# Tables and ranks within the first convolution, moved group norm parts, and logit copies between the two exponentials of a step

## The chip, the cores and the metric

The kernel runs on one core of a Trainium2 chip, all in float32. The metric is the device time of one execution in microseconds (us); before the change the median of three runs is 3284.09 us (3280.82 to 3286.93). Five engines work beside each other, each on its own list of instructions in order: TensorE (PE; PEld is its weight load), VectorE (DVE), ScalarE (ACT), GpSimd (POOL) and SyncE (SP), which here only issues DMA transfers. They wait for each other through semaphores.

## What is computed

Eight images of 512 channels by 32 x 32 pixels. A first layer normalises x in 32 groups, runs a convolutional block with two attention stages, and adds x; a second layer normalises the result, multiplies by a masked 1x1 convolution with permuted output channels, and adds again. Cut to what matters (constants in numbers, reshapes left out):

```python
def layer0(x):                       # x = x + layer0(gn(x))
    t = silu(bn(conv1x1(x, cv1_w)))
    ys = [t[:, :256], t[:, 256:]]
    for i in range(2):
        z = silu(bn(conv3x3(ys[-1], m_cv1_w[i])))
        q, k, v = conv1x1(z, m_qkv_w[i])          # 4 heads of 64, 1024 positions
        a = softmax(einsum('bhdi,bhdj->bhij', q, k + (rw + rh)) / 8)
        z = einsum('bhij,bhdj->bhdi', a, v)
        ys.append(ys[-1] + silu(bn(conv1x1(z, m_cv2_w[i]))))
    return silu(bn(conv1x1(concat(ys), cv2_w)))

def layer1(x):                       # x = x + layer1(gn(x))
    s_hat, t_hat = softmax(S, 1), softmax(T, 1)   # 512 channels x 16 groups
    s, t = argmax(s_hat, 1), argmax(t_hat, 1)
    mask = t[:, None] == s[None, :]
    w_eff = conv * t_gain[:, None] * mask         # the gains are the largest entries
    dense = conv1x1(x * s_gain, w_eff)
    p = argsort(t, stable=True)
    return dense[:, p[p]]
```

## The kernel before

**Stages.** At the start, x of the first two images is loaded and normalised and goes through the first 1x1 convolution (`start_conv`, lines 930 to 942, called in lines 943 to 957). The 3x3 convolution of the first image follows (lines 962 to 968); each third step of it also runs a piece of the generator `last_weights` (lines 608 to 699), which prepares layer 1. Its pieces: the one-hot tables of S and T and their largest entries; `oht`, the transposed tables; the mask, multiplied into the convolution weights; `rank`, the place of each channel in the stable sort; a permutation matrix from it; and two rounds of matmuls that permute the weights. For `rank`, line 668 runs 5 + 6 + 7 + 8 = 26 matmuls of 16 columns, one chain for each block of 128 channels: all "lower group" counts of four blocks, the one-hot counts of the blocks before, and a triangle within the block.

**The attention.** It is split into 64 units: image, block, pair of heads, half of the positions. A unit has 8 key tiles t; for each, `logits` (line 487) multiplies k by q into two banks `lg`, ScalarE copies the banks into a tile `st` (line 500), and VectorE takes the running maximum `mx` (line 505). After the last tile `top` (line 507) transposes the maxima (`mt`) and `spread` (line 516) transposes the negated maxima back over the partitions (`mb`). Then `soften` (line 523) adds `mb` on VectorE (line 525), takes the exponential on ScalarE (line 526) and adds the tiles up on GpSimd (`sum`, line 531); `values` (line 533) multiplies by v into `po` (line 537). `finish` (line 545) sums over the partitions by `den` and divides (line 554).

**The loop** (lines 1004 to 1034) works in steps of two key tiles on two units at once: the exponentials and values of unit u, the logits of unit u + 1. One step emits `soften(t)`, `soften(t + 1)`, `values(t - 2)`, `values(t - 1)`, next unit's `logits(t)` and `logits(t + 1)`, and then `advance`: as much filler (convolutions of other images, projections) as the planner counts for the step. The next unit's logits take their `st` tiles from a pool of ten (`stp`), so a copy into one waits until the values matmul and the sum of its former user are done. Five PSUM banks (`ps_f`) serve logits and all filler.

**What sets the order.** Each engine gets its instructions in the order in which the program emits them, as far as a scheduler keeps it; `in_turn` (line 182) fixes the order of VectorE for the attention. Nothing fixes ScalarE's order. A clock of planned times (`Clock`, line 711) is advanced by the estimated microseconds of each emitted TensorE piece; `clock.at(d, f)` emits f when d planned us have passed.

**Group norm.** `GroupNorm` (lines 134 to 166) takes statistics on VectorE; `mean` (line 141) aggregates them (`mv`), averages over a group by a matmul with `gmat` (`gm`, line 146) and forms squares (`gd`); `var` (line 154) does the second matmul (`gv`, line 156), GpSimd takes the power (`gr`), VectorE the offset (`go`). ScalarE then normalises (line 165). These parts are placed by the clock: in `First.early` (line 755) 9 and 13 us after x of a later image is asked for, in `Second.body` (line 782) 11 and 16 us after an image's last matmul of layer 0.

**Small loads.** `small_parameters` (line 561) issues five small transfers from ScalarE's queue, in the order batch norm constants (`bn_sb`), `rw`, `rh`, S and T (`s_sb`), and VectorE prepares the batch norm factors `bn_s` and `bn_b`.

Of the kernel before, what the change touches and what calls it, by code (L numbers as in the profile page):

```python
# [39 lines left out]
def conv_preact_kernel(ctx: ExitStack, tc: tile.TileContext, x, cv1, cv2, mcv1, qkv, mcv2, bn, rw, rh, conv, s_in, t_in, out):  # L40
# [141 lines left out]
    def in_turn(instruction):  # L182

        if turn:
            tc.add_manual_dep(instruction.ins, turn.pop().ins.name, IN_ORDER, reason="order of VectorE")
        turn.append(instruction)

    class Spread:

# [288 lines left out]
    class Unit:  # L478
# [8 lines left out]
        def logits(self, t):  # L487

            if t == 0:
                self.begin()  # L490
            lg = [bank(f"lg_{self.name}_{t}_{h}") for h in range(2)]
            for h in range(2):
                r = slice(HD * h, HD * h + HD)
                nc.tensor.matmul(  # L494
                    lg[h], self.k[r, ts(t, P)], self.q[r, self.hp, ts(self.half, HALF)], start=True, stop=True
                )
            st = pair(stp, "st", f"st_{self.name}_{t}")
            self.st.append(st)
            for h in range(2):
                nc.scalar.copy(st[:, h], lg[h])  # L500
            if t == 1:
                self.mx = pair(one, "mx", f"mx_{self.name}")
            for h in range(2 if t else 0):
                so_far = self.st[0] if t == 1 else self.mx
                in_turn(nc.vector.tensor_tensor(self.mx[:, h], so_far[:, h], lg[h], ALU.max))  # L505
# [17 lines left out]
        def soften(self, t):  # L523
            st = flat(self.st[t])
            in_turn(nc.vector.tensor_tensor(st, st, flat(self.mb), ALU.add))  # L525
            nc.scalar.activation(st, st, AF.Exp)  # L526
            if t == 1:
                self.acc = pair(one, "acc", f"sum_{self.name}")
            for h in range(2 if t else 0):
                so_far = self.st[0] if t == 1 else self.acc  # L530
                nc.gpsimd.tensor_tensor(self.acc[:, h], so_far[:, h], self.st[t][:, h], ALU.add)  # L531
# [28 lines left out]

    def small_parameters():

        nc.scalar.dma_start(out=bn_sb, in_=bn)
        nc.scalar.dma_start(out=rw_sb, in_=rw)
        nc.scalar.dma_start(out=rh_sb, in_=rh)
        nc.scalar.dma_start(out=s_sb[:, 0], in_=s_in)
        nc.scalar.dma_start(out=s_sb[:, 1], in_=t_in)
        nc.vector.tensor_scalar_add(bn_b, bn_sb[:, 3], 1e-3)
        nc.gpsimd.tensor_tensor(bn_s, bn_b, mhalf, ALU.pow)
        nc.vector.tensor_tensor(bn_s, bn_s, bn_sb[:, 0], ALU.mult)  # L570
        nc.vector.tensor_tensor(bn_b, bn_sb[:, 2], bn_s, ALU.mult)
        nc.vector.tensor_tensor(bn_b, bn_sb[:, 1], bn_b, ALU.subtract)
# [35 lines left out]
    def last_weights():  # L608

        weff = [pair(stp, "st", f"weff_{j}") for j in range(2)]  # L610
        for j in range(2):
            load(weff[j], conv[:, 2 * j : 2 * j + 2])
        scr = flat(pair(stp, "st", "scr")).rearrange("p (a k g) -> p a k g", a=8, g=NG)
        gi = scr[:, 0]
        gi_i = scr[:, 7].bitcast(mybir.dt.int32)
        nc.gpsimd.iota(gi_i, pattern=[[0, 2 * CT], [1, NG]], base=-NG, channel_multiplier=0)
# [22 lines left out]
        nc.vector.tensor_tensor(oh, gi, wide(idx), ALU.is_equal)  # L639
        nc.vector.tensor_tensor(lower, gi, wide(idx), ALU.is_gt)  # L640

        yield
        oht = pair(stp, "st", "oht")[:NG]
        for a in range(2):
            ps = bank(f"oht_{a}")
            for k in range(CT):
                nc.tensor.transpose(ps[:NG, ts(k, P)], oh[:, CT * a + k], ident)
            nc.vector.tensor_copy(oht[:, a], ps[:NG])
        yield
        for k in range(CT):  # L650
            ps = bank(f"mask_{k}")
# [2 lines left out]
            stt(wk, wk, gain[:, CT + k : CT + k + 1], ps, ALU.mult, ALU.mult)  # L654

        yield

        tri = small.tile([P, P], F32, tag="tri", bufs=1, name="tri")
        nc.gpsimd.affine_select(
            out=tri, in_=ones, pattern=[[1, P]], compare_op=ALU.is_gt, fill=0.0, base=0, channel_multiplier=-1  # L660
        )
        rank = small.tile([P, CT], F32, tag="rank", bufs=1, name="rank")
        for k in range(CT):
            ps = bank(f"rank_{k}")
            terms = [(ones, lower[:, CT + c]) for c in range(CT)] + [(ones, oh[:, CT + c]) for c in range(k)]
            terms.append((tri, oh[:, CT + k]))
            for n, (w, rhs) in enumerate(terms):
                nc.tensor.matmul(ps[:, :NG], w, rhs, start=(n == 0), stop=(n == len(terms) - 1))
            nc.vector.tensor_tensor(e[:, k], ps[:, :NG], oh[:, CT + k], ALU.mult)
        nc.vector.tensor_reduce(rank, e[:, :CT], AX.X, ALU.add)  # L670

        io = pair(stp, "st", "io")
        io_i = io[:, 1].bitcast(mybir.dt.int32)
        nc.gpsimd.iota(io_i, pattern=[[1, HALF]], base=0, channel_multiplier=0)
# [76 lines left out]
    class First(Item):  # L751
# [4 lines left out]
        def early(self):  # L756
            if self.h == 0:
                self.im.measure_x()
                clock.at(9.0, self.im.gn0.mean)
                clock.at(13.0, self.im.gn0.var)  # L760
                self.im.normed = clock.now + 13.0

        def setup(self):
            self.tiles = self.im.load_x(self.h)
# [8 lines left out]
    class Second(Item):  # L773
# [8 lines left out]
        def body(self):  # L782
            yield from self.im.conv2(self.h, self.tiles)
            if self.h == 1:
                clock.at(11.0, self.im.gn1.mean)
                clock.at(16.0, self.im.gn1.var)
                self.im.normed = clock.now + 16.0
                self.im.measured = True
                bg.prepare()

# [160 lines left out]
    clock.at(9.0, second.gn0.var)  # L951
    clock.at(11.0, lambda: start_norm(second, tiles2))
    clock.at(12.0, lambda: transform_weights(0))
    clock.run(start_conv(first, tiles, w))
    first.load_y()
    bg.add(*(First(m, h) for m in images[2:] for h in range(2)))
# [2 lines left out]
    positions(0)  # L959
    bg.prepare()  # L960
    first.transform(0, 0.0, 0.0)
    side = last_weights()
    for n, us in enumerate(first.conv3(0)):
        clock.tick(us)
        if n % 3 == 0:
# [15 lines left out]
    for s in range(len(slots)):  # L981
# [22 lines left out]
        for j in range(4):  # L1004
# [91 lines left out]
```

## Time and profile before

| | |
|---|---|
| median of three runs | 3284.09 us (3280.82 to 3286.93) |
| profiled execution, its own time | 3278.47 us |
| its span in the trace | 3276.7 us |
| mean granted TensorE clock | 0.99 of full speed |
| logit copies (line 500) | 1024 of 594 ns |
| exponentials (line 526) | 512 of 1056 ns |
| sums on GpSimd (line 531) | 768 of 1299 ns, 128 of 1288 ns |
| logits, values (lines 494, 537) | 2048 records each, 618 and 609 ns |
| first convolution matmul starts | 18.61 us |
| transfers | 399.30 MB, 122 GB/s on average |

How to read it: "busy" is the time in which an engine executed; a group of instructions is given with the count, the mean of one in ns, and the idle time of the engine just ahead of them with what ended it (`<-`). `out<-in` names the tiles. L505 is line 505 of the kernel. PEclk is the clock that TensorE was granted, 1 being full speed; a matmul at 0.5 takes twice as long. An engine's idle time costs only where the work that ends last waits for it. A matmul in float32 shows as two records.

### The profile page before, as it was taken

The numbers are of one execution on the slowest core, as the hardware profiler recorded it, in microseconds if no ns is written. First come the engines' busy times: TensorE is split into PE (matmuls) and PEld (weight loads), VectorE is DVE, ScalarE is ACT, GpSimd is POOL, SyncE is SP. The second block draws the span as 40 slices with busy tenths as digits, with TensorE's granted clock in tenths as the row PEclk, the third lists the DMA queues.
The fourth block names the chain that finished last, engine by engine and source line by source line (L and its number), as shares of the span: only waits on it lengthen the run. The fifth ranks groups of instructions, "written<-read, shape, count | busy, mean of one in ns | idle before, by whom it ended". The sixth has DMA issues, their size and how long they took to land.

```text
span 3276.7 us, 33257 instructions
## 1 busy us (share of the span) xinstructions
PE 3159.1 (96%) x11716; PEld 1538.0 (47%) x11716; DVE 2045.9 (62%) x2717; ACT 1756.6 (54%) x2369; POOL 1219.1 (37%) x971
## 2 busy tenths in 40 slices
PE   7999999998999999999999999999999999999998
PEld 3645345353545445354545445354445444453343
DVE  5436566666666575767666675767656676666642
ACT  3245765854545655644545555644655554646631
POOL 2104433335334343344334343444334433444420
PEclk9999999999999999999999999999999999999999
DMA  8752352330323241423323341423333341423366
GB/s 292 275 171 71 119 170 94 116 106 20 121 98 106 75 148 55 161 84 106 122 98 105 104 144 54 161 84 108 124 105 108 101 141 49 160 71 116 111 217 205
DMA packets 142007, 399.30 MB, mean 122 GB/s; under 512 B 13072, under 2 KB 14352, under 8 KB 141840
## 3 DMA queue, kind: packets, MB, share of 16 engines
q1 hardware_dynamic: 141120, 396.94, 36.1%
q8 instruction: 93, 1.52, 0.2%
q14 instruction: 74, 0.61, 0.1%
q10 hardware_dynamic: 720, 0.23, 0.0%
HBM read 317.42 MB, written 79.69 MB: 121 GB/s over the span
## 4 chain that ended last, share of the span: by engine, by line
PE 69%; DVE 11%; issue 5%; ACT 4%; DMA 4%; POOL 1%; POOLq 0%; SPq 0%; ACTq 0%; DVEq 0%
PE cv L175 14%; PE m L297 12%; PE po L537 11%; PE lg L494 10%; PE qk L175 6%; PE l L175 5%; PE v L389 3%; DVE st L525 3%; PE mt L513 2%; PE m L175 2%; DVE rb L556 2%; DVE mx L505 2%; PE den L549 2%; PE mb L521 2%; DMA x<-in_x 1%
## 5 line engine op out<-in xcount | busy, mean ns | idle before, releaser
L531 POOL TENSOR_TENSOR sum<-sum,st 128x512 f32<-128x512 f32 x768 | 973.9, 1299 | 771.5 <-ACT st L526 771.5
L526 ACT ACTIVATE st<-st 128x1024 f32<-128x1024 f32 x512 | 534.3, 1056 | 471.4 <-DVE st L525 464.8
L505 DVE TENSOR_TENSOR mx<-mx,lg 128x512 f32<-128x512 f32 x768 | 479.3, 681 | 434.1 <-ACT st L500 433.6
L500 ACT COPY st<-lg 128x512 f32<-128x512 f32 x1024 | 528.1, 594 | 246.1 <-PE lg L494 189.9
L525 DVE TENSOR_TENSOR st<-st,mb 128x1024 f32<-128x1024 f32 x512 | 604.2, 1213 | 79.8 <-PE mb L521 79.8
L297 PE MATMUL m<-plane,w_m 128*128 128x256 f32 x2304 | 534.0, 386 | 18.0 <-DVE z L351 8.3
L494 PE MATMUL lg<-q,k 64*128 64x512 f32 x2048 | 534.6, 618 | 10.4 <-ACT rb L551 3.3
L537 PE MATMUL po<-st,v 128*64 128x512 f32 x2048 | 509.5, 609 | 17.2 <-ACT st L526 11.4
L297 PEld LDWEIGHTS m<-plane,w_m 128*128 128x128 f32 x2304 | 431.4, 191 | 142.7 <-issue 40.8
L531 POOL TENSOR_TENSOR sum<-st,st 128x512 f32<-128x512 f32 x128 | 162.2, 1288 | 834.1 <-ACT st L526 712.0
L175 PE MATMUL cv<-y,w_cv 128*128 128x512 f32 x1024 | 466.5, 600 | 4.9 <-DVE mx L505 2.1
L494 PEld LDWEIGHTS lg<-q,k 64*128 64x128 f32 x2048 | 188.9, 186 | 346.2 <-issue 236.5
L175 PEld LDWEIGHTS cv<-y,w_cv 128*128 128x128 f32 x1024 | 185.5, 190 | 252.0 <-issue 231.6
L537 PEld LDWEIGHTS po<-st,v 128*64 128x64 f32 x2048 | 125.2, 136 | 327.6 <-issue 231.6
L556 DVE RECIPROCAL rb<-rb 128x256 f32<-128x256 f32 x128 | 216.1, 1725 | 66.0 <-ACT rb L551 66.0
L175 PE MATMUL cv<-x,w_cv 128*128 128x512 f32 x512 | 242.2, 622 | 12.3 <-DVE mx L505 4.1
L175 PE MATMUL l<-x,w_l 128*128 128x512 f32 x512 | 235.2, 604 | 9.6 <-DVE mx L505 6.2
L175 PE MATMUL qk<-z,w_qkv 128*128 128x512 f32 x512 | 234.2, 600 | 1.6 <-DVE mx L505 1.6
L514 DVE TENSOR_REDUCE nm<-mt 128x4 f32<-128x512 f32 x128 | 83.0, 685 | 221.5 <-PE mt L513 221.2
L130 ACT ACT_TABLE_LOAD x122 | 156.5, 1283 | 14.7 <-PE m L175 6.4
L175 PEld LDWEIGHTS cv<-x,w_cv 128*128 128x128 f32 x512 | 97.0, 197 | 138.7 <-issue 112.1
L175 PEld LDWEIGHTS l<-x,w_l 128*128 128x128 f32 x512 | 93.3, 191 | 133.6 <-issue 106.5
(144 smaller groups left out, 2342.1 us busy)
## 6 DMA issues: line engine op xcount, KB each, us to landing
w_m<-w_m SPq DMA_DIRECT2D x96, 768.0 KB, 4.4
w_cv<-in_cv SPq DMA_DIRECT2D x90, 512.0 KB, 3.5
y<-y SPq DMA_DIRECT2D x64, 512.0 KB, 4.7
x<-in_x SPq DMA_DIRECT2D x56, 512.0 KB, 5.2
y<-y SPq DMA_DIRECT2D x64, 256.0 KB, 3.6
k<-r SPq DMA_DIRECT2D x32, 512.0 KB, 3.8
res<-y SPq DMA_DIRECT2D x32, 512.0 KB, 4.2
xr<-in_x SPq DMA_DIRECT2D x32, 512.0 KB, 4.3
```

The costliest lines, as they stand in the source:

```text
L130: nc.scalar.activation(dst, src, AF.Silu, bias=bn_b[:, col : col + 1], scale=bn_s[:, col : col + 1])
L175: nc.tensor.matmul(ps, w, moving, start=(n == 0), stop=(n == len(terms) - 1))
L297: nc.tensor.matmul(ps[:, ts(co, 256)].rearrange("p (t x) -> p t x", x=F), w[:, co, c, dx], u[:, 9 * c : 9 * c + 8, dx : dx + F], start=(j ...
L389: nc.tensor.matmul(ps[:, ts(j, P)], z[:, c, ts(4 * j4 + j, P)], w[:, c, 512 + P * hp : 512 + P * hp + P], start=(c == 0), stop=(c == IT - 1),)
L494: nc.tensor.matmul(lg[h], self.k[r, ts(t, P)], self.q[r, self.hp, ts(self.half, HALF)], start=True, stop=True)
L500: nc.scalar.copy(st[:, h], lg[h])
L505: in_turn(nc.vector.tensor_tensor(self.mx[:, h], so_far[:, h], lg[h], ALU.max))
L525: in_turn(nc.vector.tensor_tensor(st, st, flat(self.mb), ALU.add))
L526: nc.scalar.activation(st, st, AF.Exp)
L531: nc.gpsimd.tensor_tensor(self.acc[:, h], so_far[:, h], self.st[t][:, h], ALU.add)
L537: nc.tensor.matmul(self.po[HD * h : HD * h + HD], self.v[:, t, ts(h, HD)], self.st[t][:, h], start=(t == 0), stop=(t == KT - 1),)
L556: nc.vector.reciprocal(self.rb[:, r], self.rb[:, r])
```

## The change

Five edits:

- Ahead of the attention, the tables of S and T, their transposes and the ranks leave `last_weights` for a generator `tables`, of which the clock emits one part 14 and one 26 planned us into the first image's first convolution. Its scratch tiles come from the pool `gr` (two buffers, idle at that time) instead of `stp`. `last_weights` takes gain, oht and rank as arguments and keeps the loads of the weights, the mask, the permutation and the two rounds of matmuls.
- The ranks are two accumulating matmuls of 64 columns. The counts that the 22 matmuls with `ones` summed are first added up on VectorE (`pre`, one reduction and three additions).
- S and T are loaded ahead of the batch norm constants.
- The group norm parts of later images move from 9 and 13 to 12 and 16 planned us; those of layer 1 move, for the last image alone, from 11 and 16 to 5 and 8.
- `soften` is split. The exponential and the sums become `exponent`. In a step with t > 0, exponent(t) comes before the values and the next unit's logits, exponent(t + 1) after them; in the step with t = 0 both come after the logits. `act_turn` fixes ScalarE's order of copies and exponentials to that of emission.

```diff
+    def act_turn(instruction):
+
+        if act_last:
+            tc.add_manual_dep(instruction.ins, act_last.pop().ins.name, IN_ORDER, reason="order of ScalarE")
+        act_last.append(instruction)
...
-                nc.scalar.copy(st[:, h], lg[h])
+                act_turn(nc.scalar.copy(st[:, h], lg[h]))
...
             in_turn(nc.vector.tensor_tensor(st, st, flat(self.mb), ALU.add))
-            nc.scalar.activation(st, st, AF.Exp)
+
+        def exponent(self, t):
+            st = flat(self.st[t])
+            act_turn(nc.scalar.activation(st, st, AF.Exp))
...
+        nc.scalar.dma_start(out=s_sb[:, 0], in_=s_in)
+        nc.scalar.dma_start(out=s_sb[:, 1], in_=t_in)
         nc.scalar.dma_start(out=bn_sb, in_=bn)
         nc.scalar.dma_start(out=rw_sb, in_=rw)
         nc.scalar.dma_start(out=rh_sb, in_=rh)
-        nc.scalar.dma_start(out=s_sb[:, 0], in_=s_in)
-        nc.scalar.dma_start(out=s_sb[:, 1], in_=t_in)
...
-        scr = flat(pair(stp, "st", "scr")).rearrange("p (a k g) -> p a k g", a=8, g=NG)
+        scr = flat(pair(gr, "gr", "scr")).rearrange("p (a k g) -> p a k g", a=8, g=NG)
...
+        pre = scr[:, 4]
+        nc.vector.tensor_reduce(pre[:, 0], lower[:, CT:].rearrange("p c g -> p g c"), AX.X, ALU.add)
+        for k in range(1, CT):
+            nc.vector.tensor_tensor(pre[:, k], pre[:, k - 1], oh[:, CT + k - 1], ALU.add)
         yield
-        oht = pair(stp, "st", "oht")[:NG]
+        oht = pair(gr, "gr", "oht")[:NG]
...
+        nc.tensor.matmul(ps, ones, pre[:, :CT], start=True, stop=False)
+        nc.tensor.matmul(ps, tri, oh[:, CT:], start=False, stop=True)
+        nc.vector.tensor_tensor(e[:, :CT], ps, oh[:, CT:], ALU.mult)
+        nc.vector.tensor_reduce(rank, e[:, :CT], AX.X, ALU.add)
...
-        for k in range(CT):
-            ps = bank(f"rank_{k}")
-            terms = [(ones, lower[:, CT + c]) for c in range(CT)] + [(ones, oh[:, CT + c]) for c in range(k)]
-            terms.append((tri, oh[:, CT + k]))
-            for n, (w, rhs) in enumerate(terms):
-                nc.tensor.matmul(ps[:, :NG], w, rhs, start=(n == 0), stop=(n == len(terms) - 1))
-            nc.vector.tensor_tensor(e[:, k], ps[:, :NG], oh[:, CT + k], ALU.mult)
-        nc.vector.tensor_reduce(rank, e[:, :CT], AX.X, ALU.add)
...
-                clock.at(9.0, self.im.gn0.mean)
-                clock.at(13.0, self.im.gn0.var)
-                self.im.normed = clock.now + 13.0
+                clock.at(12.0, self.im.gn0.mean)
+                clock.at(16.0, self.im.gn0.var)
+                self.im.normed = clock.now + 16.0
...
-                clock.at(11.0, self.im.gn1.mean)
-                clock.at(16.0, self.im.gn1.var)
-                self.im.normed = clock.now + 16.0
+                mean, var = (11.0, 16.0) if self.im.n < NB - 1 else (5.0, 8.0)
+                clock.at(mean, self.im.gn1.mean)
+                clock.at(var, self.im.gn1.var)
+                self.im.normed = clock.now + var
...
+    ranks = tables()
+    clock.at(14.0, lambda: next(ranks))
+    clock.at(26.0, lambda: next(ranks))
     clock.run(start_conv(first, tiles, w))
...
-    side = last_weights()
+    side = last_weights(*table_results)
...
                 u.soften(t + 1)
                 if t:
+                    u.exponent(t)
                     u.values(t - 2)
                     u.values(t - 1)
                     clock.tick(2.0)
                 if nxt:
                     nxt.logits(t)
                     nxt.logits(t + 1)
                     clock.tick(2.0)
+
+                if not t:
+                    u.exponent(t)
+                u.exponent(t + 1)
                 advance((base + 4 + t) / steps)
```

More of the change, by code (lines that the diff above doesn't have):

```diff
@@ L186, in in_turn @@
         turn.append(instruction)
+    def act_turn(instruction):
+        if act_last:
+            tc.add_manual_dep(instruction.ins, act_last.pop().ins.name, IN_ORDER, reason="order of ScalarE")
+        act_last.append(instruction)
+    act_last = []
     class Spread:
@@ L606, in transform_weights, with tables @@
                 load(w_m1[i][r][:, co].rearrange("p c t o -> p (c t o)"), t)
[L608 to L612, printed above, removed]
-        scr = flat(pair(stp, "st", "scr")).rearrange("p (a k g) -> p a k g", a=8, g=NG)
+    table_results = []
+    def tables():
+        scr = flat(pair(gr, "gr", "scr")).rearrange("p (a k g) -> p a k g", a=8, g=NG)
         gi = scr[:, 0]
@@ L648, in last_weights @@
             nc.vector.tensor_copy(oht[:, a], ps[:NG])
+        tri = small.tile([P, P], F32, tag="tri", bufs=1, name="tri")
+        nc.gpsimd.affine_select(
+            out=tri, in_=ones, pattern=[[1, P]], compare_op=ALU.is_gt, fill=0.0, base=0, channel_multiplier=-1
+        )
+        rank = small.tile([P, CT], F32, tag="rank", bufs=1, name="rank")
+        ps = bank("rank").rearrange("p (k g) -> p k g", g=NG)[:, :CT]
+        nc.tensor.matmul(ps, ones, pre[:, :CT], start=True, stop=False)
+        nc.tensor.matmul(ps, tri, oh[:, CT:], start=False, stop=True)
+        nc.vector.tensor_tensor(e[:, :CT], ps, oh[:, CT:], ALU.mult)
+        nc.vector.tensor_reduce(rank, e[:, :CT], AX.X, ALU.add)
+        table_results.extend((gain, oht, rank))
+        yield
+    def last_weights(gain, oht, rank):
+        weff = [pair(stp, "st", f"weff_{j}") for j in range(2)]
+        for j in range(2):
+            load(weff[j], conv[:, 2 * j : 2 * j + 2])
         yield
@@ L656, in last_weights @@
         yield
[L658 to L662, printed above, removed]
-        for k in range(CT):
-            ps = bank(f"rank_{k}")
-            terms = [(ones, lower[:, CT + c]) for c in range(CT)] + [(ones, oh[:, CT + c]) for c in range(k)]
-            terms.append((tri, oh[:, CT + k]))
-            for n, (w, rhs) in enumerate(terms):
-                nc.tensor.matmul(ps[:, :NG], w, rhs, start=(n == 0), stop=(n == len(terms) - 1))
-            nc.vector.tensor_tensor(e[:, k], ps[:, :NG], oh[:, CT + k], ALU.mult)
-        nc.vector.tensor_reduce(rank, e[:, :CT], AX.X, ALU.add)
         io = pair(stp, "st", "io")
```

## The prediction

> **What bounds the kernel now.** First the page: shares of the engines, then the costliest groups.
>
> ```profile
> PE 3159.1 (96%) x11716; PEld 1538.0 (47%) x11716; DVE 2045.9 (62%) x2717; ACT 1756.6 (54%) x2369; POOL 1219.1 (37%) x971
> L505 DVE TENSOR_TENSOR mx<-mx,lg 128x512 f32<-128x512 f32 x768 | 479.3, 681 | 434.1 <-ACT st L500 433.6
> L500 ACT COPY st<-lg 128x512 f32<-128x512 f32 x1024 | 528.1, 594 | 246.1 <-PE lg L494 189.9
> L526 ACT ACTIVATE st<-st 128x1024 f32<-128x1024 f32 x512 | 534.3, 1056 | 471.4 <-DVE st L525 464.8
> L531 POOL TENSOR_TENSOR sum<-sum,st 128x512 f32<-128x512 f32 x768 | 973.9, 1299 | 771.5 <-ACT st L526 771.5
> L130 ACT ACT_TABLE_LOAD x122 | 156.5, 1283 | 14.7 <-PE m L175 6.4
> ```
>
> TensorE is the bound: 96%. No other engine passes 62%, so the 446.9 us that VectorE waits for logit copies, or what ScalarE waits for its adds, cost nothing by themselves. Only three things can shorten the run: TensorE's waits, its slow stretches, and work taken off it. The waits are next (engine, line, what it waited for: us, times, longest):
>
> ```profile
> PE gm_a L146 <- DVE mv_a L144: 19.8, 3, 14.2
> PE po L537 <- ACT st L526: 11.4, 6, 4.4
> PE mt L513 <- DVE mx L505: 10.7, 3, 3.6
> PE m L175 <- ACT st L500: 4.0, 6, 0.7
> PE l L175 <- ACT x L165: 3.4, 3, 2.9
> PE lg L494 <- ACT st L500: 3.0, 5, 1.7
> PE lg L494 <- ACT y L130: 3.1, 1, 3.1
> PE m L297 <- DMA w_m<-w_m: 2.8, 2, 1.8
> ```
>
> All of TensorE's waits of the attention (242 to 3180 us) add to about 81 us in 72 waits; that is the ceiling there. Third, windows behind the longer stalls (us; busy time of PE, PEld, DVE, ACT, POOL with counts; PEclk; DMA share; GB/s):
>
> ```profile
> 101.40:108.30 6.90, 6.90 (x26) 6.27 (x26) 4.01 (x11) 1.85 (x3) 0.00 (x0) 0.51 0.15 43
> 224.30:231.10 6.80, 5.93 (x15) 3.79 (x16) 1.38 (x8) 3.18 (x5) 0.00 (x0) 0.50 0.54 207
> 432.50:439.40 6.90, 6.63 (x8) 2.55 (x9) 6.18 (x7) 5.75 (x9) 2.50 (x2) 0.51 0.10 38
> 3242.00:3245.00 3.00, 3.00 (x4) 1.27 (x5) 0.00 (x0) 1.90 (x4) 0.00 (x0) 0.50 0.94 261
> ```
>
> TensorE is busy there but at half clock: a stall is paid again, by 1.7 us (3.4 us at half speed) or 3.4 us. Fourth, the timeline of TensorE at the two places the change names (start, duration, instruction, [idle before <- releaser]):
>
> ```profile
> 97.40 1.04 PE L668 MATMUL rank<-scr,ones 128*128 128x16 f32 x8
> ...
> 101.42 3.15 PE L668 MATMUL rank<-scr,ones 128*128 128x16 f32 x14
> 104.40 0.59 PE L668 MATMUL rank<-scr,tri 128*128 128x16 f32 x2
> 104.83 5.82 PE L297 MATMUL m<-plane,w_m 128*128 128x256 f32 x18
> ...
> 3241.76 4.49 PE L175 MATMUL l<-x,w_l 128*128 128x512 f32 x6 [2.86 <-ACT x L165]
> ```
>
> **What the Trainium skill says.** "TensorE: Matmul & The Clock Gate", Part 1, gives TensorE two clocks, the lower at half speed after an idle window of about 3.4 us and the higher after about 3.4 us of activity. The trace agrees on the sizes (stretches at 0.50 of 3.4 and 6.9 us), but here waits as short as 1.52 us (588.09) and a run of tiny rank matmuls precede them. "PSUM — Partial Sum Buffer", Terms, says that two engines may not touch one bank at once, reads included; the trace agrees in that the max of a logits bank waits for its copy (446.9 us). So a late copy delays both the max and the release of the bank.
>
> **The change part by part.**
>
> *Copies ahead of the second exponential.* Now each step of ScalarE runs exp(t), exp(t+1), then four copies of the next unit's logits; a copy whose matmul is done stands behind an exp that waits for VectorE's add, and a table load (1283 ns) may stand with it. Afterwards it is exp(t), copies, exp(t+1). I went through each TensorE wait of the attention and looked at what ScalarE was doing. Waits that end with a copy behind an exp: m<-st 0.67 x6; lg<-st 0.31 x4 and 1.73 (3006.77); l<-mx 1.34, 0.58, 1.35; cv<-mx 0.70 x3, and three of 1.78, 0.34 and 0.73 at 468 to 545. Sum 15.2 us. I book 10, since something else may be late next. Waits behind table loads (copies, a silu and exps alternating): 2.17 at 396.97, 3.08 at 432.77, 1.89 at 647.39 and 0.42 x3, 8.4 us, and with half clock 1.7 + 3.4 + 1.7 = 6.8 more, 15.2 in all; the changed order of instructions has 114 table loads for 122 and fewer silus between two exps. I book 8. Untouched: mt<-mx 3.57 x3, whose start is a VectorE wait for a DMA, the m<-z waits of the convolution planes, the po waits at 775 to 792 (VectorE and POOL), 5.8 us of po<-q.
>
> What it costs: exp(t+1) now starts after the copies. I measured the room, from the end of the last logits matmul of a step to the start of po(t+1): median 6.2 us, tenth percentile 5.0 at t=0 and 3.6 at t=6. Needed are the wait for the last copy, the copy (0.6), exp (1.06) and about 0.2 of handing over, together 2.1, or 3.4 with a table load. Five of 504 cases fall short, by 4.9 us in sum. POOL starts its sums later too; the last one must be ready for the den matmul, and the copies of step 2 need the buffer that the sums of tiles 0 and 1 give back. The sums take 5.2 to 7 us of a step's 9 to 10; the tenth percentile of the room (7.1) is inside their latest end (7.9), so between 0 and 8 us are lost there. Together I take +5 from a range of 0 to +20.
>
> *Group norm parts.* The first image of the next pair is measured 3 us later on the planner's clock. That takes VectorE's statistics, which wait for x to land, out of the way of the max at 360.50 (2.53 + 1.7), and gives room at 421.94 (1.38) and 588.09 (1.52 + 1.7): 8.8. At 225.17 the same part waits 4.23 us (second of the three gm_a waits) and half clock costs 3.4; 3 planned us later the transfers, which land by 225.5, are mostly there; half of 7.6, 3.8. Sum 12.6; I book 9 (bounds 4 and 16.4).
>
> *Last image's parts earlier, 5 and 8 for 11 and 16.* Nothing but 64 l matmuls is left there. Now gm_b starts at 3236.68 because VectorE is held 4.38 us by a residual's DMA (L471 at 3236.8); normalised x is ready at 3241.7. Planned 6 us sooner, the chain goes ahead of that residual and gv's 8 us sooner, so norm_x starts near 3235.3, before its user is due at 3238.3. Gone: 2.86, 0.28 for gm/gv behind the matmuls, 1.7 of half clock: 5 (bounds 3 and 6).
>
> *Tables within the first convolution, ranks by two matmuls.* 26 rank matmuls (52 records) run 97.40 to 104.83 = 7.43 us, then 18 m matmuls take 5.82 against 4.05 at full clock elsewhere in that loop, 1.8. Eight transposes for oht are 1.04. Two matmuls of 64 columns I put at 0.45 (16-column pairs take about 0.13 us of pitch each, and 512 columns 0.43). The 1.5 us move into first's or second's first convolution, where they end before the transformed weights' DMA, for which TensorE waits 1.84 and 0.95 us at 78.23 and 85.47: they are filled, not added. So −7.4 −1.8 −1.0, and nothing added: −10.3 (bounds 7 and 12). The table operations of VectorE, one more than before, lie in a convolution where it is mostly idle.
>
> *S and T loaded first.* The tables' reduce waits 2.37 us for T at 9.79, ahead of the last statistics; T will land by about 6.3. But the batch norm constants, whose add precedes the statistics in VectorE's queue, go from first to third, landing at about 7.8 for 2.6, and some table operations get in between the statistics and gm_a. The chain to the first cv (18.61) thus loses about what it gains: +1 (0 to +2).
>
> *Sum.* −10 −8 −9 −5 −10.3 +5 +1 = −36.3. On the profiled run, 3278.5 (span 3276.7 and 1.8 around it), this is 3242. The median of the runs is 5.6 above the profiled one, so 3284.1 − 36.3 = 3247.8; I say 3247.
>
> **Rivals.**
>
> A: the stalls of the attention don't go, because VectorE, a DMA or POOL is late next; the new costs eat what goes. For it: the adds themselves are what exps wait for (464.8). Against it: the fixable waits above end on a finished matmul and a busy ScalarE. Then tables and tail alone: −10.3 −5 +1 = −14.3, 3270.
>
> B: everything goes, half clocks too: −15.2 −15.2 −16.4 −6 −12 +1 = −64, 3220. For it: many of the stalls recur in the same place of every image pair. Against it: so much order changes that new stalls are likely.
>
> C, slower: the chain of step 2. exp(1) later, so sums of tiles 0 and 1 later, so the buffer later, so the copies of logits 2 and 3 and TensorE behind them. It recurs in 63 units. Gains with all but this chain's own term are 41.3; from 0.66 us per unit it decides, and at 0.85 us (53.5 in sum) the time is 3284 + 12 = 3296. For it: POOL's 771.5 us of waiting for exps, and 41.3 us (18 waits) in which copies already wait for a sum. Against it: the median room of 9.1 us.
>
> D: the moved norm parts only shift their waits (no −9) and the start loses 2: 3257, within the range.
>
> **How the numbers follow.** The forecast with D 0.60, A 0.20, B 0.09, C 0.11. Its own range is 3232 to 3262; with A and most of B, 3226 to 3275 leaves out C and the rest of B. What is under 0.2% (6.6 us) can't be told from no change in this kernel; A with larger new costs gives most of that. Faster 0.84, same 0.06, slower 0.10.
>
> **What would show it.** Right: no rank group at 97 us, the m matmuls behind it at full clock, the wait of l<-x in the tail gone or below 1 us, gm_a's second and third wait gone, m<-st and lg<-st waits gone, fewer than 122 table loads. Wrong: more po<-st (exp) waits than 6, copies waiting for sums well over 41 us, new lg waits in step 2 of every unit, or a first cv later than 20.6.

## The result, and the profile after

The changed kernel takes 3248.72 us (median of four runs, 3244.98 to 3251.55). The ratio to the kernel before is 0.9903 with an interval of 0.989 to 0.9916; on 3280 us that is 27.5 to 36 us, 32 in the middle. The profiled execution took 3244.98 us with a span of 3243.3.

First the page of the changed kernel, its shares and groups. Line numbers have moved: the copies are L508, the maxima L513, the adds L533, the exponentials L537, the sums L542.

```profile
PE 3141.8 (97%) x11668; PEld 1519.6 (47%) x11668; DVE 2071.7 (64%) x2718; ACT 1727.1 (53%) x2353; POOL 1243.3 (38%) x971
L542 POOL TENSOR_TENSOR sum<-sum,st 128x512 f32<-128x512 f32 x768 | 993.8, 1319 | 719.2 <-ACT st L537 719.1
L513 DVE TENSOR_TENSOR mx<-mx,lg 128x512 f32<-128x512 f32 x768 | 477.6, 682 | 370.2 <-ACT st L508 370.1
```

There are 48 TensorE records fewer (52 of the ranks against 4), and VectorE waits 370 us for copies where it waited 434. The single operations last about as long as before (of those listed before, a sum differs most: 1319 ns for 1299). TensorE's waits over the whole span (engine, line, what it waited for: us, times, longest), cut to eight of 24 lines:

```profile
PE gm_a L146 <- DVE bn_s L581: 13.2, 1, 13.2
PE po L548 <- ACT st L537: 12.6, 12, 2.9
PE cv L175 <- DVE mx L513: 9.7, 8, 2.1
PE m L305 <- ACT cv2s L130: 8.4, 3, 3.0
PE po L548 <- DVE q L569: 7.6, 8, 2.5
...
PE mt L521 <- DVE mx L513: 2.7, 4, 0.8
...
PE m L305 <- DMA w_m<-w_m: 0.8, 1, 0.8
...
PE l L175 <- ACT x L165: 0.4, 2, 0.2
```

All 24 lines together are 95.0 us, where the list of the kernel before adds to 111.1. Of gm_a only the wait at the start is left; no line has m or lg waiting for a copy any more (4.0 and 3.0 before); l<-x in the tail is 0.4 for 3.4; mt<-mx is 2.7 for 10.7. New are three waits of m for cv2s (8.4). One kind did not shrink: apart from mt, TensorE waited for the maxima mx in 20 places for 22.0 us, and now does in 21 for 26.1. The timeline of TensorE where the ranks used to run:

```profile
77.70 5.42 PE L305 MATMUL m<-plane,w_m 128*128 128x256 f32 x24 [0.85 <-DMA w_m<-w_m]
83.06 3.69 PE L686 MATMUL mask<-oht 16*128 16x512 f32 x8
86.68 9.71 PE L305 MATMUL m<-plane,w_m 128*128 128x256 f32 x36
96.23 0.28 PE L146 MATMUL gm_a<-mv_a,gmat 128*128 128x4 f32 x2
96.37 7.11 PE L703 MATMUL w<-weff,perm 128*128 128x512 f32 x16
103.32 4.05 PE L305 MATMUL m<-plane,w_m 128*128 128x256 f32 x18
```

No rank group stands there, and 18 m matmuls take 4.05 us where 5.82 were seen. The ranks now run inside the first convolution, as two matmuls:

```profile
47.91 1.04 PE L662 MATMUL oht<-ident,scr 128*16 128x128 f32 x8
48.78 0.33 PE L671 MATMUL rank<-scr,ones 128*128 128x64 f32 x2
48.95 0.39 PE L672 MATMUL rank<-scr,tri 128*128 128x64 f32 x2
```

To see where the time came from I compared the two traces at fixed places in the program, by the start of a unit's first logits matmul. The difference of after and before (us): first convolution matmul −0.6, first logits (183.9 before) −9.9, unit 8 (576.8) −20.2, unit 16 −27.7, unit 32 −32.9, unit 61 −35.5, unit 62 −29.8, last unit's den matmul −29.7, end −33.4. So a third comes ahead of the attention, most of the rest in the first image pair (up to unit 16), and something is given back between units 61 and 62. These are two single executions: a second profile of the kernel before (below) is itself 6.0 us ahead of the first from unit 16 on, so a difference of that size need not come from the change.

### The profile page after: what moved, and what is told of

Same layout as the page of the kernel before. It is cut to its first block, busy times and chain, and to the rows that moved or that the text cites. A ratio compares the mean times of both kernels' runs of the same rounds, so it can differ in the third digit from the quotient of the medians.

```text
span 3243.3 us, 33195 instructions
## 1 busy us (share of the span) xinstructions
PE 3141.8 (97%) x11668; PEld 1519.6 (47%) x11668; DVE 2071.7 (64%) x2718; ACT 1727.1 (53%) x2353; POOL 1243.3 (38%) x971
## 4 chain that ended last, share of the span: by engine, by line
PE 72%; DVE 11%; ACT 5%; DMA 4%; issue 3%; POOL 0%; SPq 0%; ACTq 0%; DVEq 0%
PE cv L175 14%; PE m L305 14%; PE po L548 12%; PE lg L502 11%; PE qk L175 6%; PE l L175 5%; PE v L397 3%; DVE st L533 2%; DVE rb L567 2%; PE mt L521 2%; PE den L560 2%; PE mb L529 2%; DVE mx L513 2%; PE m L175 1%; DMA x<-in_x 1%
## 5 line engine op out<-in xcount | busy, mean ns | idle before, releaser
L542 POOL TENSOR_TENSOR sum<-sum,st 128x512 f32<-128x512 f32 x768 | 993.8, 1319 | 719.2 <-ACT st L537 719.1
L537 ACT ACTIVATE st<-st 128x1024 f32<-128x1024 f32 x512 | 540.8, 1069 | 390.9 <-DVE st L533 389.8
L513 DVE TENSOR_TENSOR mx<-mx,lg 128x512 f32<-128x512 f32 x768 | 477.6, 682 | 370.2 <-ACT st L508 370.1
L533 DVE TENSOR_TENSOR st<-st,mb 128x1024 f32<-128x1024 f32 x512 | 604.9, 1214 | 71.3 <-PE mb L529 71.3
L508 ACT COPY st<-lg 128x512 f32<-128x512 f32 x1024 | 524.4, 596 | 228.0 <-PE lg L502 222.8
L548 PE MATMUL po<-st,v 128*64 128x512 f32 x2048 | 514.2, 611 | 20.4 <-ACT st L537 12.6
L542 POOL TENSOR_TENSOR sum<-st,st 128x512 f32<-128x512 f32 x128 | 168.0, 1334 | 847.5 <-ACT st L537 807.2
L175 PE MATMUL cv<-x,w_cv 128*128 128x512 f32 x512 | 233.8, 603 | 8.6 <-ACT x L165 2.4
L562 ACT COPY rb<-den 128x512 f32<-128x512 f32 x64 | 37.4, 584 | 233.7 <-PE den L560 233.3
L175 PEld LDWEIGHTS qk<-z,w_qkv 128*128 128x128 f32 x512 | 93.6, 191 | 130.8 <-issue 95.9
```

The lines of the kernel that those rows point to most:

```text
L175: nc.tensor.matmul(ps, w, moving, start=(n == 0), stop=(n == len(terms) - 1))
L508: act_turn(nc.scalar.copy(st[:, h], lg[h]))
L537: act_turn(nc.scalar.activation(st, st, AF.Exp))
L548: nc.tensor.matmul(self.po[HD * h : HD * h + HD], self.v[:, t, ts(h, HD)], self.st[t][:, h], start=(t == 0), stop=(t == KT - 1),)
```

## The experiments

In each run the kernel shown is set against runs of the kernel before on the same chip. One part of the change at a time comes first, then pairs and parts taken away, then a few questions that these left. The parts of the last image and the order of the small loads have no run of their own. "TensorE's waits" without more is the sum over the whole list of them in the profiled execution; two profiles of the kernel before give 111.1 and 111.0 us, so this sum varies less than the time.

### The split of the exponentials alone

```diff
-            nc.scalar.activation(st, st, AF.Exp)
+        def exponent(self, t):
+            act_turn(nc.scalar.activation(st, st, AF.Exp))
...
+                    u.exponent(t)
                     u.values(t - 2)
...
+                if not t:
+                    u.exponent(t)
+                u.exponent(t + 1)
                 advance((base + 4 + t) / steps)
```

> The kernel before with the split of soften and act_turn alone. Theory (copies stood behind an exponential that had to wait): the waits m<-st copy (6 of 0.67 us) and lg<-st copy are gone, with some of those behind table loads; 10 + 8 us gained and 5 given back, so 13 us faster than before (8 to 20), ratio near 0.996. Rival A (something else is late next): within 4 us of before. Rival C (the later exponential delays sums and copies of step 2): slower by 10 us or more, with copies waiting for sums far above 41 us.

Measured: 3276.2 us, ratio 0.9989 (0.9978 to 1.0000), so 3.6 us (0 to 7) where 13 were expected. The waits that the theory named did go, but others stood in their place. Waits of TensorE of this kernel, cut to four:

```profile
PE gm_a L146 <- DVE mv_a L144: 21.7, 3, 14.2
PE po L548 <- ACT st L537: 17.4, 12, 2.8
PE cv L175 <- DVE mx L513: 9.8, 8, 2.0
...
PE m L305 <- ACT cv2s L130: 8.5, 3, 3.0
```

The third of these in the kernel before:

```profile
PE cv L175 <- DVE mx L505: 6.2, 6, 2.5
```

No m or lg waits for a copy any more (7.0 us before). But the waits of TensorE for mx apart from mt, of which the prediction booked 8.2 us as copies behind an exponential, are 24.4 us in 21 places for 22.0 in 20; po waits for exponentials rose from 11.4 to 17.4; and the group norm's waits are about what they were. In sum TensorE waits 110.7 us, for 111.1.

### The order fixed, but exponentials first

```diff
-            nc.scalar.activation(st, st, AF.Exp)
+            act_turn(nc.scalar.activation(st, st, AF.Exp))
...
-                nc.scalar.copy(st[:, h], lg[h])
+                act_turn(nc.scalar.copy(st[:, h], lg[h]))
```

> The kernel before with act_turn on copies and exponentials, in the old order of emission: both exponentials ahead of the copies. Theory (the order between copies and the second exponential counts): no gain, within 4 us of before, and m<-st copy and lg<-st copy still wait. Rival (it is the fixing of ScalarE's order, and fewer table loads, that helps): at least half of what the split alone brings, 6 us or more, and fewer than 122 table loads.

Measured: 3294.86 us, ratio 1.0049 (1.0032 to 1.0066). No gain, as expected, but 16 us slower instead of within 4. Table loads (L130) are 123, not fewer than 122, so the rival is out. I counted in how many of the 252 steps both exponentials run ahead of all four copies: 196 in the kernel before, 252 in this one, none in the split. So the kernel before was not a kernel with copies behind exponentials throughout: in 56 steps its scheduler had already put at least one copy ahead. Between two kernels whose order is fixed, from 252 to none is worth 18.7 us (3294.86 to 3276.2). That the scheduler had already found the copies that matter most, and left the split only the rest, fits these numbers but is not shown; nor is the way from the order to the 16 us, since TensorE's waits are only 113.0 us for 111.1 in this profile and half clock costs 44.0 us for 32.8, in an execution that is the slowest of its six (3300.78).

### The group norm parts of later images alone

```diff
-                clock.at(9.0, self.im.gn0.mean)
-                clock.at(13.0, self.im.gn0.var)
+                clock.at(12.0, self.im.gn0.mean)
+                clock.at(16.0, self.im.gn0.var)
```

> The kernel before with the group norm parts of later images at 12 and 16 planned us alone. Theory: the stalls at 225, 360, 422 and 588 us go or shrink: 9 us faster (4 to 16). Rival D (the waits only move to other places): within 3 us of before, with waits of like sum on gm_a, gv_a or on the maxima elsewhere.

Measured: 3279.9 us, ratio 0.9999 (0.999 to 1.0009). Nothing, where 9 us were expected. The waits at the stall near 225 us show it, each cut to one line. Before, then the split alone, then the moved parts alone, then the changed kernel:

```profile
PE gm_a L146 <- DVE mv_a L144: 4.2, 1, 4.2
```

```profile
PE gm_a L146 <- DVE mv_a L144: 3.8, 1, 3.8
```

```profile
PE gv_a L156 <- ACT st L500: 3.6, 1, 3.6
```

```profile
PE gv_a L156 <- ACT st L508: 0.9, 1, 0.9
```

With the parts moved alone, gm_a no longer waits for the statistics, but gv_a, the next matmul of the chain, waits 3.6 us, now for a copy on ScalarE. With both mended 0.9 us is left (0.7 in the kernel of the next section). ScalarE shows why, first with the parts moved alone, then with the split too:

```profile
232.74 2.00 ACT L526 ACTIVATE st<-st 128x1024 f32<-128x1024 f32 x2
234.64 2.03 ACT L500 COPY st<-lg 128x512 f32<-128x512 f32 x4
```

```profile
230.65 1.52 ACT L165 ACTIVATE x<-x,go_a,gr_a 128x512 f32<-128x512 f32 x2 [2.23 <-issue]
232.08 2.02 ACT L508 COPY st<-lg 128x512 f32<-128x512 f32 x4
```

In the first, both exponentials, behind a table load of 1.28 us, stand ahead of the copies, which clear the banks that TensorE needs next, and gv_a starts at 235.26. In the second the copies follow the normalisation at once, and gv_a starts at 232.69. One stall had two causes, and neither edit alone removes it.

### The two together

> The kernel before with two parts: split and act_turn, and the group norm parts of later images at 12 and 16. Alone they brought ratios of 0.9989 and 0.9999. Theory of interaction (each stall of the first image pair has two causes, the late copy and the late group norm part, and goes only when both are mended): 11 to 15 us faster than before, ratio near 0.996, idle and half-clock time of TensorE before 650 us well below that of either alone. Rival (parts add): 4 us faster, ratio 0.9988.

Measured: 3268.04 us, ratio 0.9966 (0.9954 to 0.9979): 11 us (7 to 15), three times what the two bring apart (3.6 + 0.3). TensorE's waits over the span are 99.7 us here, 110.7 and 113.1 with one part alone, 111.1 before. Between 180 and 660 us they are 21.9 here, 25.6 and 29.5 with one part alone, 26.9 before.

### The changed kernel without one of them

> The changed kernel without the split and act_turn. Theory of interaction: 12 to 16 us slower than the changed kernel, ratio to before 0.994 to 0.995. Rival (parts add): 4 us slower than it, ratio 0.9914.

> The changed kernel with the group norm parts of later images back at 9 and 13. Theory of interaction: 8 to 11 us slower than the changed kernel, ratio to before 0.993 to 0.994, stalls and half clock again near 215, 410 and 575 us. Rival (parts add): the same as the changed kernel within 3 us, ratio 0.990 to 0.991.

Measured: without the split 3258.71 us, ratio 0.9936 (0.9923 to 0.9948); without the moved parts 3259.23 us, ratio 0.9939 (0.9921 to 0.9958). Against 0.9903 each takes away 11 to 12 us, with an uncertainty of 6 to 8. TensorE's waits between the first logits and the last den matmul, the stage that the two parts change, say the same in two families of kernels:

| TensorE's waits in the attention, us | neither | split alone | moved parts alone | both |
|---|---|---|---|---|
| old tables and ranks | 86.0 | 84.8 | 86.2 | 73.8 |
| tables and ranks moved | 80.3 | 80.8 | 81.6 | 74.5 |

(The second row is the tables alone, the changed kernel without the moved parts, without the split, and whole.) So both give their gain only with the other, from whichever side it is looked at. The rival, that parts add, is out.

### The changed kernel without the fixed order

```diff
-                act_turn(nc.scalar.copy(st[:, h], lg[h]))
+                nc.scalar.copy(st[:, h], lg[h])
...
-            act_turn(nc.scalar.activation(st, st, AF.Exp))
+            nc.scalar.activation(st, st, AF.Exp)
```

> The changed kernel without act_turn: the order of emission is kept, the fixed order of ScalarE is gone. Fixing it alone made the kernel before 15 us slower. Theory (the fixing costs by itself, the place of the exponential gains): 8 to 15 us faster than the changed kernel, ratio to before 0.986 to 0.988. Rival (without it the scheduler puts exponentials ahead of copies again): 4 us slower than the changed kernel or more, with m<-st copy and lg<-st copy waits back.

Measured: 3262.25 us, ratio 0.9955 (0.9941 to 0.9969), some 17 us slower than the changed kernel. The rival holds: in 127 of 252 steps both exponentials are ahead of all copies again, although the later one is emitted behind them. TensorE's waits are 114.7 us for 95.0; lg waits for copies again (2.0 us in 5), m does not. The wait that grew most:

```profile
PE l L175 <- DVE mx L513: 14.5, 5, 4.0
```

It is 7.7 in the changed kernel. The order has to be fixed, but only fixing the right order pays.

### Tables and ranks alone

The edit is the part of the change from `tables` to `last_weights(*table_results)`.

> The kernel before with the tables moved into the first convolution and the ranks by two matmuls alone. Theory: 10 us faster (7 to 12), first logits matmul 10 us earlier than 183.9, all of it before 110 us. Rival (the work that moves is paid in the first convolution, where TensorE waits for the tables of VectorE): 6 us or less, with the first convolution's end later than 76.4 by 2 us or more.

Measured: 3263.25 us, ratio 0.995 (0.9933 to 0.9967): 16 us (11 to 22), more than the 10 expected. In the trace the first logits matmul comes 7.8 us earlier and the first convolution matmul 0.9 later, so 8.7 us are won between them; the rest of this execution's gain lies in the attention.

### The ranks by two matmuls, left in place

```diff
-        for k in range(CT):
-            ps = bank(f"rank_{k}")
-            terms = [(ones, lower[:, CT + c]) for c in range(CT)] + [(ones, oh[:, CT + c]) for c in range(k)]
...
+        nc.tensor.matmul(ps, ones, pre[:, :CT], start=True, stop=False)
+        nc.tensor.matmul(ps, tri, oh[:, CT:], start=False, stop=True)
```

> The kernel before with the ranks by two matmuls of 64 columns, the tables left where they are. Theory (the ranks are the work that goes, with the half clock behind them): first logits matmul at about 175.5 for 183.9, 8 to 9 us faster than before, ratio near 0.9975. Rival (most of the 16 us that tables and ranks brought together came from taking the tables out of the 3x3 convolution): 4 us or less.

Measured: 3263.32 us, ratio 0.9955 (0.9943 to 0.9968), 15 us. The first logits come only 3.8 us earlier, where 8 to 9 were expected. The timeline of TensorE shows what became of the rest:

```profile
85.55 1.04 PE L647 MATMUL oht<-ident,scr 128*16 128x128 f32 x8
86.42 4.05 PE L297 MATMUL m<-plane,w_m 128*128 128x256 f32 x18
90.31 0.28 PE L146 MATMUL gm_a<-mv_a,gmat 128*128 128x4 f32 x2
90.52 4.12 PE L652 MATMUL mask<-oht 16*128 16x512 f32 x8
94.57 7.06 PE L297 MATMUL m<-plane,w_m 128*128 128x256 f32 x18
...
101.61 0.41 PE L668 MATMUL rank<-scr,ones 128*128 128x64 f32 x2
101.86 0.39 PE L669 MATMUL rank<-scr,tri 128*128 128x64 f32 x2
102.08 4.11 PE L297 MATMUL m<-plane,w_m 128*128 128x256 f32 x18
```

The ranks themselves are 0.5 us for 7.4, and the m matmuls behind them run at full speed. But 18 m matmuls behind the mask take 7.06 us: half clock stands there now. All six profiles with the old ranks have 6.8 us of it at the ranks, none of the eight with the new ones; but seven of these eight have some behind the mask, which only two of the six have.

So the two kernels win 3.8 and 7.8 us before the attention and 12 and 9 between there and the last den matmul, although from the first logits on they list the same instructions in the same order as the kernel before on every computing engine; of what the traces list only the queue of transfers differs, in the first 110 or so of 790 entries (buffer numbers are left out there, so another place in memory is not excluded). In that stage TensorE's waits are 80.9 and 80.3 us for 86.0, and half clock costs 18.8 and 25.6 for 27.3. The second profile of the kernel before, at the fast end of its runs, is 6.7 us shorter in this stage too, all of it half clock (20.5), with waits of 85.7. The clearest single difference is a wait of m for z, 2.12 us at 1051 before (2.11 in its second profile) and in neither of the two. It ends after two additions of the residual on VectorE. Before, then the ranks in place:

```profile
1046.06 3.20 DVE L414 TENSOR_TENSOR res<-res,m2s 128x512 f32<-128x512 f32 x2 [1.51 <-issue]
```

```profile
1032.05 1.29 DVE L414 TENSOR_TENSOR res<-res,m2s 128x512 f32<-128x512 f32 x2 [0.60 <-issue]
```

Before, the idle time ahead of the two additions is 0.9 us longer, and the additions take 1.9 us longer; a second profile of the kernel before (below) has 2.24 and 2.47 there, and the two new kernels have 0.57 and 0.60, and 1.29. What makes these additions late is not settled. The sums say where the surplus lies, in waits and in half clock, and not why.

### The kernel before, beside itself

> The kernel before, unchanged, beside itself. Theory (half-clock stretches stand on a grid of 3.41 us whose phase differs between executions, so a stall is punished by 0, 1.7, 3.4 or 5.1 us at random): ratio 1.000 within 0.0015; the same stalls in the profile to 0.1 us where no transfer is concerned, but half-clock stretches of other lengths or places, their loss off by 2 us or more. Rival (they belong to the kernel): the same stretches at the same places.

Measured: ratio 1.0004 (0.9996 to 1.0013), medians 3281.2 and 3279.01 with single runs from 3272 to 3287. In the second profile the stalls of the attention are the same ones, most to 0.1 us, but the clock answers otherwise. The window of the second profile at the gm_a stall (columns as in the prediction):

```profile
224.30:231.10 6.80, 5.68 (x17) 3.23 (x18) 2.63 (x9) 3.35 (x5) 0.00 (x0) 0.75 0.66 245
225.20:228.60 3.40, 3.18 (x6) 1.66 (x7) 0.72 (x6) 1.52 (x2) 0.00 (x0) 0.50 0.94 348
```

A stall of 3.85 us is followed by 3.4 us of half clock here; in the first profile 4.23 us are followed by 6.8. The stretches at 398, 589 and 647 us are missing altogether. Over the span half clock costs 32.8 us in the first profile and 26.0 in the second; the second one's span is 3270.6 for 3276.7, and the difference of 6.0 is close to the 6.8 of the clock. In each of the fourteen profiles all stretches of one execution start on one grid of 3.4133 us, whose offset differs from one execution to the next (2.45 us in the first profile of the kernel before, 1.35 in that of the changed kernel).

### Other places for the exponentials

First, exponential 0 goes ahead of the copies in the step with t = 0 too:

```diff
+                u.exponent(t)
                 if t:
-                    u.exponent(t)
...
-                if not t:
-                    u.exponent(t)
                 u.exponent(t + 1)
```

> The changed kernel with exponential 0 ahead of the copies in the step with t = 0 too (63 of 252 steps), exponential 1 behind them as now. Theory (an exponential ahead of copies costs; from all 252 steps behind to none it was 18.6 us): 2 to 6 us slower than the changed kernel. Rival (the late start of the first exponential and sum costs more in this step): 2 to 6 us faster, with fewer po waits for exponentials.

Measured: 3264.17 us, ratio 0.9957 (0.9945 to 0.9969), 17 to 18 us slower than the changed kernel, far above the 2 to 6 expected. The groups of this kernel and of the changed one show a difference beside the copies:

```profile
L130 ACT ACT_TABLE_LOAD x129 | 165.5, 1283 | 14.6 <-PE m L175 6.4
L537 ACT ACT_TABLE_LOAD x128 | 164.2, 1283 | 2.2
```

```profile
L130 ACT ACT_TABLE_LOAD x114 | 146.3, 1283 | 8.4 <-PE m L175 6.4
L537 ACT ACT_TABLE_LOAD x113 | 145.0, 1283 | 2.0
```

Exponentials of one step that stand apart let a silu in between, which costs a load to the silu and one back: 30 loads more, 38 us of ScalarE. The Trainium skill, "ScalarE: Activation LUTs", Rules for kernel authors, advises doing all of one table set before switching. Of its price for a switch, some 2.7 us, the traces show 1.28 us, and the next function starts 0.013 us after the load in the median. In this kernel lg waits 4.09 us at 425.77 for a silu behind such a pair of loads; the changed kernel's stall there is 1.41. ScalarE is not the bound, so its 38 us are not the loss: TensorE's waits are 101.8 us for 95.0, and half clock costs 28.8 for 18.4, part of which can be chance. How much the loads cost and how much the copies is not separated.

Second, the later exponential goes between the two pairs of copies (with t = 0 the earlier one does):

```diff
                     nxt.logits(t)
+                if not t:
+                    u.exponent(t)
+                else:
+                    u.exponent(t + 1)
+                if nxt:
                     nxt.logits(t + 1)
...
-                if not t:
-                    u.exponent(t)
-                u.exponent(t + 1)
+                if not t:
+                    u.exponent(t + 1)
```

> The changed kernel with the later exponential between the two pairs of copies of a step (for t = 0 the first of the two, the second stays last). Theory (copies behind an exponential that waits for VectorE hold the maxima and TensorE): 4 to 9 us slower than the changed kernel. Rival (the 12 po waits for exponentials, 12.6 us with half clock behind them, count more): 3 to 8 us faster.

Measured: 3245.5 us, ratio 0.9897 (0.9884 to 0.9909). The interval overlaps that of the changed kernel (0.989 to 0.9916): neither of the two expectations is borne out; it beats the kernel before, but that it beats the changed one is not shown. Its trace has both effects at once, and they cancel: the sum of TensorE's waits is 95.0 us in both. Waits of TensorE:

```profile
PE l L175 <- DVE mx L513: 16.8, 5, 5.5
...
PE po L548 <- ACT st L537: 2.7, 9, 0.5
```

po<-exponential falls from 12.6 to 2.7, and l<-mx rises from 7.7 to 16.8.

## Why the prediction was right, and where its steps were not

The time was right (3247 forecast, 3248.72 measured), but partly by luck. One term was 11 us too large, another some 6 too small. And the sum started from 3284.1, the median of three runs, where later sets of runs of the same kernel have medians of 3279.01 to 3281.2: the gain booked was 36.3 us, the one measured 32 (27.5 to 36).

**Copies ahead of the second exponential, −10 −8 +5, and group norm parts, −9.** Together −22 booked, −11 (7 to 15) measured. The step that failed is that each TensorE wait was given one cause and booked to one edit. At the 225 us stall the statistics and a copy were both late, and neither edit alone removes it. And 8.2 of the 15.2 us booked as a copy behind an exponential were waits for a maximum; with the copies ahead the waits for maxima are not fewer (22.0 us before, 24.4 with the split alone, 26.1 in the changed kernel). Here rival A was right: something else is late next. Rival D, that moved parts only shift their waits, was right of the moved parts alone (3.6 us to gv_a) and wrong of the whole. A reading was wrong too, though the sum, taken from waits, does not rest on it: the old order is not exp, exp, copies in every step; the scheduler had a copy ahead in 56 of 252. Part of the mechanism stands: the waits of m and lg for a copy are gone, table loads (L130) went from 122 to 114 as the listing said, and the kernel that puts all exponentials ahead is 16 us slower.

**The added cost, +5 (0 to +20).** No run has this cost by itself. The waits it was read from are small in the changed kernel: po waits for exponentials became 12 for 6, a sign named for being wrong, but 12.6 us for 11.4. Rival C is refuted: copies waiting for a sum went from 41.3 us in 18 waits to 4.6 us in 8.

**What was called untouched.** mt<-mx did not stay at 10.7 us; it fell to 2.7, and three waits of m for cv2s of 2.6 to 3.0 us, 8.4 in all, took its place. For the sum this made little difference, but the step was wrong. Both stand in the split alone too (3.8 and 8.5), so it is the order of ScalarE that reaches further than the waits that end on a copy.

**Tables and ranks, −10.3 (7 to 12).** Ahead of the attention 8.7 us came (9.3 in the changed kernel, first convolution matmul to first logits), inside the bounds. The cost of the two ranks, 0.45 booked, was 0.5 (of its parts, 0.13 us is near the pitch of one record, 0.11; a matmul of 16 columns is two). The half clock did go with the ranks, but some came back behind the mask (3.4 us long in the changed kernel, 6.8 with the ranks left in place), which no step had. On the whole run the part brings 16 us (11 to 22) instead of 10, and the 6 to 7 beyond come from a stage which the change doesn't touch; for this surplus the traces show differences, but no cause is shown.

**The tail, −5.** From the last den matmul to the end the changed kernel is 3.7 us shorter. The other five kernels with this part are 3.0 to 6.0 shorter, the six without it, apart from the kernel before, between 1.4 shorter and 2.3 longer. So about 4 to 5: right in size. One reading in it was wrong: gm_b did not start late because VectorE was held. Its input was ready at 3229.3, and TensorE reached it in its order at 3236.68, without a wait; the residual at 3236.80 then held the step behind it. Planned earlier, gm_b follows its input within 0.6 us.

**The start, +1.** The first convolution matmul came 0.6 us earlier. With the tables alone it comes 0.9 later, and in the kernels that load S and T first too between 0.1 and 0.6 earlier. But in the kernels where nothing changed at the start it lies between 0.5 earlier and 0.6 later. So the +1 did not show, and a gain by the load order is likely but not shown.

**Given back.** Between units 61 and 62 the changed kernel loses 5.7 us. A wait of 2.45 us stands there, of po for the division of the unit before, and 6.8 us of half clock behind it (3.4 us lost):

```profile
2972.87 1.08 PE L548 MATMUL po<-st,v 128*64 128x512 f32 x4 [2.45 <-DVE q L569]
```

That is 5.85 us; VectorE's two reciprocals before it take 3.36 us. The wait also occurs without the moved parts, with the split alone, with both of these, and with the later exponential between the copies (2.45 us each); in this last one no half clock follows it.

**Rival B**, that everything goes, half clock too, was too hopeful: half clock lost 32.8 us in the profile before, 18.4 after, and since two profiles of one kernel differ by 6.8, a part of this can be chance.

## What to carry to other kernels

A stall of the bound engine (here TensorE) that two late inputs share is not won by mending either; before adding up the gains of parts, ask of each stall what would be late next, and test the parts in pairs. In this kernel an order that was written down paid only when it was fixed, and fixing the wrong one cost: the same pins gave 16 us more or 17 less, depending on what stood first. The exponential that was moved apart from its neighbour brought 30 table loads more; count them before moving one that could start earlier.

## What was not expected of the hardware

- A stall's price depends on the execution: half-clock stretches are multiples of 3.41 us (the last is cut off by the end of the trace) on a grid whose offset changes from run to run. The same stall was followed by 6.8 us and by 3.4 us of half clock, others, like the 2.12 us at 1051 before, by none, and the same program's span differed by 6.0 us with it.
- TensorE can be busy by the record and still be slowed: about where 3.7 to 4.1 us of mask matmuls end, which fill 16 of 128 rows, the clock went to 0.50 in nine of fourteen profiles (86.7 to 90.1 us in the changed kernel, with no wait longer than 0.85 us in the 9 us ahead of it). That the mask is the cause is not tested.
